# Borders of 256 in TensorE's instruction stream and the order of SyncE's transfers, in a multi-query attention kernel

## The chip, the cores and the metric

The kernel runs on one core of one Trainium2 chip. The metric is the time of one execution in device microseconds; before the change it is the median of three runs. All data are fp32.

## What is computed

64 batches of 128 tokens with 512 channels pass through a residual attention layer with 16 heads of 64 channels that share one set of keys and values (multi-query), plus one null key and value:

```python
xn = layernorm(x, g_in)
q = (xn @ Wq).reshape(b, n, H, DH).transpose(0, 2, 1, 3) * scale
k, v = split(xn @ Wkv)                    # one head for all
k = concatenate([null_kv[0], k]); v = concatenate([null_kv[1], v])
sim = einsum('bhid,bjd->bhij', q, k) + bias     # causal, then key mask
attn = softmax(sim)
out = einsum('bhij,bjd->bhid', attn, v) @ Wo
return x + layernorm(out, g_out)
```

The inputs are x (64 x 128 x 512), a bias of 16 x 128 x 128, the null key and value, a mask of 64 x 128, both gains and the weights Wq (512 x 1024), Wkv (512 x 128) and Wo (1024 x 512).

## The kernel before

The order of the instructions is written out by hand (`tc.manual_schedule()`): each engine executes its instructions in the order in which the Python code records them. Semaphore waits between engines and for buffers are put in by the framework. SyncE (SP) issues nearly all DMAs, in program order too: where one of its DMAs has to wait, those behind it wait as well.

The batches are worked on in pairs. `cycle(c)` (c from 1 to 33) mixes the stages of several pairs, with b0 = 2c:

- softmax of the pair b0, b0 + 1, whose scores the cycle before left (`scores_max`, `exps`, `rinv`, `scale`, `blocks_T`);
- output products of the pair p = b0 - 2 (`out_one`), and normalization, gain, residual and `store` of the pair r = b0 - 4;
- query products of a group two cycles ahead (`q_one`) and keys and values of batches b0 + 6 and b0 + 7 (`key_values`);
- statistics, normalization and transposition of the tokens of the batches m = b0 + 10 and m + 1 (`norm_stats`, `norm_apply`, `tokens_T`);
- at its end `region(c)`: the scores of the next pair (`heads`, L539, 64 small matmuls in program terms) and the values of the present pair (`values`, L648, 56 of them). On TensorE the region is one run of short instructions between stretches of large products.

Query and output products use Strassen's scheme with seven products (numbered 1 to 7; 4 is the last), spread over the cycle. An fp32 matmul of the program is four TensorE instructions: two weight loads and two matmuls. A full cycle has 64 + 56 + 28 + 28 + 8 matmuls (scores, values, queries, output, keys and values), so 736 such instructions, and about six separate semaphore waits. Query products end with cycle 29, keys and values with cycle 28.

Four batches form a group (GB = 4) for transfers that change the layout. They go out to DRAM and come back in another shape:

- `tokens_out` (L335, xd<-xb) and `tokens_in` (L343, xT<-xd, four DMAs) for the transposed tokens;
- `keys_T`: a VectorE transpose (kb), then L396 kd<-kb, and four DMAs L402 kT<-kd;
- `values_spread`: L379 vd<-kvt, and four DMAs L383 vr<-vd.

Each of these functions issues the way out and the way back one behind the other, so that SyncE stands at the way back until the way out has landed. All of them are called at the end of even cycles, ahead of `region(c)`, together with `load_mask`; the residual loads (`load_res`, two buffers) and the next token loads (`load_x`, three buffers) are called there in every cycle. The output tiles y have three buffers, so the DVE addition that fills a y half (L755) waits until an older y has been stored (L797).

## Time and profile before

| | |
|---|---|
| runs | 1105.44, 1102.42, 1107.50 us; median 1105.44 |
| profiled execution, its own time | 1109.08 us |
| span from the first to the last instruction in it | 1107.3 us |
| mean granted TensorE clock | 0.986 |
| busy: TensorE, VectorE, ScalarE, GpSimd | 1050.6, 764.0, 679.3, 708.0 us |
| DMA | 105.05 MB, mean 95 GB/s |
| instruction packets on q8 | 93 of together 1.52 MB |

The page gives busy times for each engine, and the chain of work that ended last. A row of the windows view is: stretch in us from the span's start, its length, then busy us and number of instructions for PE (TensorE's matmuls), PEld (its weight loads), DVE (VectorE), ACT (ScalarE) and POOL (GpSimd), then the granted clock, the mean busy share of the DMA engines and GB/s. A row of the timeline is: start, length, engine, line, operation, tiles written and read, and in brackets the idle time before it and what ended it. A row of the source view gives a count and the shortest, median and longest time in ns, and the first and last start in us. PEldq is TensorE's sequencer, SPq SyncE's.

### The profile page before, as it was taken

Reading aid. Unit: us, or ns where it says so; the run is one execution under the profiler, and the core shown is the slowest. Engines: PE = TensorE matmul, PEld = TensorE weight load, DVE = VectorE, ACT = ScalarE, POOL = GpSimd, SP = SyncE. Lnnn points to the kernel's source line nnn. Section 1 sums busy time; section 2 is a strip of 40 time slices with the busy share of each in tenths; the row PEclk is TensorE's granted clock in tenths of the full one; section 3 lists DMA queues with packets and bytes.
Section 4 is the critical chain, followed back from the end, with each engine's and each line's share of the span. In section 5 each row is a group of like instructions: output and inputs, shape, how many; then the busy total and the mean of one; then the engine's idle time right before and its main releaser. Section 6 shows DMA issues by size and latency. Waiting matters only on the chain.

```text
span 1107.3 us, 30317 instructions
## 1 busy us (share of the span) xinstructions
PE 1050.6 (95%) x11856; PEld 908.5 (82%) x11856; DVE 764.0 (69%) x1654; ACT 679.3 (61%) x2822; POOL 708.0 (64%) x530
## 2 busy tenths in 40 slices
PE   9999999999999999999999999999999999999765
PEld 8888888787888888888887888887888887888554
DVE  6776766667677777776777777776776676666563
ACT  3656567654677665567664667765557764556662
POOL 3786576484776767577574766757576575656642
PEclk9999999998999999999999999999999999999899
DMA  6641241413315042241514324142341504111111
GB/s 202 158 125 53 97 133 52 138 49 121 110 52 164 32 140 85 97 136 50 147 48 129 95 82 142 50 128 68 115 118 62 157 26 136 50 66 51 39 39 58
DMA packets 68686, 105.05 MB, mean 95 GB/s; under 512 B 8640, under 2 KB 32832, under 8 KB 66752
## 3 DMA queue, kind: packets, MB, share of 16 engines
q1 hardware_dynamic: 67440, 102.08, 30.1%
q8 instruction: 93, 1.52, 0.6%
q10 hardware_dynamic: 1104, 1.05, 0.3%
q14 instruction: 49, 0.40, 0.1%
HBM read 67.45 MB, written 35.65 MB: 93 GB/s over the span
## 4 chain that ended last, share of the span: by engine, by line
PE 76%; ACT 9%; DMA 5%; DVE 4%; issue 3%; SPq 1%; POOL 0%; DVEq 0%; ACTq 0%; POOLq 0%
PE pa L485 15%; PE pyX L736 15%; PE ps L539 8%; PE pc L485 8%; PE pyY L736 8%; ACT s L587 5%; PE poX L648 4%; PE pw L485 4%; PE pkv L354 4%; PE pyw L736 3%; PE pos L648 2%; DMA out_dram<-y 2%; PE pq L434 2%; DMA kd<-kb 2%; PE poY L648 2%
## 5 line engine op out<-in xcount | busy, mean ns | idle before, releaser
L587 ACT ACTIVATE s<-s,nmax 128x65 f32<-128x65 f32 (+1 forms) x1024 | 376.7, 389 | 0.0
L523 POOL TENSOR_TENSOR s<-biasp,mneg 128x1552 f32<-128x1552 f32 x64 | 206.1, 3221 | 66.1 <-DVE sb L623 61.9
L608 POOL TENSOR_TENSOR s<-s,rinv 128x512 f32<-128x512 f32 (+1 forms) x128 | 190.5, 1488 | 48.3 <-DVE rinv L604 47.7
L587 ACT ACTIVATION_READ_ACCUMULATOR s<-s,nmax 128x1 f32 x1024 | 217.6, 213 | 0.0
L719 POOL TENSOR_TENSOR yS<-oT 128x512 f32<-128x512 f32 x32 | 40.8, 1274 | 178.0 <-ACT oT L679 178.0
L679 ACT ACTIVATE oT<-poX,nv 128x256 f32<-128x256 f32 x64 | 30.4, 475 | 186.3 <-PE poX L648 105.6
L573 DVE TENSOR_TENSOR s<-ps,s 128x256 f32<-128x256 f32 (+2 forms) x224 | 119.9, 606 | 26.1 <-PE ps L539 23.8
L623 DVE STREAM_TRANSPOSE sb<-s 128x1536 f32<-128x1536 f32 x64 | 113.4, 1773 | 32.6 <-POOL s L608 32.4
L736 PE MATMUL pyX<-wo,oT 128*128 128x256 f32 x512 | 121.4, 380 | 6.0 <-ACT oT L679 3.9
L736 PE MATMUL pyX<-wT,oT 128*128 128x256 f32 x512 | 122.2, 382 | 5.1 <-POOL oT L719 5.1
L485 PE MATMUL pa<-xS,wq 128*128 128x256 f32 x480 | 123.4, 379 | 0.5 <-ACT ku L496 0.5
L578 DVE TENSOR_REDUCE nmax<-s 128x8 f32<-128x520 f32 (+1 forms) x128 | 116.2, 949 | 0.0
L736 PEld LDWEIGHTS pyX<-wo,oT 128*128 128x128 f32 x512 | 96.9, 190 | 21.1 <-ACT oT L679 5.3
L736 PEld LDWEIGHTS pyX<-wT,oT 128*128 128x128 f32 x512 | 97.9, 192 | 19.8 <-POOL oT L719 6.3
L648 PE MATMUL pos<-sb,vr 32*64 32x128 f32 (+1 forms) x1792 | 90.9, 325 | 8.5 <-issue 8.5
L485 PEld LDWEIGHTS pa<-xS,wq 128*128 128x128 f32 x480 | 88.9, 190 | 11.8 <-ACT ku L496 0.9
L539 PEld LDWEIGHTS ps<-kT,qT 64*64 64x64 f32 x4096 | 85.4, 134 | 10.4 <-issue 10.3
L539 PE MATMUL ps<-kT,qT 64*64 64x128 f32 (+1 forms) x4096 | 93.1, 245 | 0.0
L506 DVE TENSOR_TENSOR qT<-pc,ku 128x256 f32<-128x256 f32 x120 | 50.4, 420 | 59.1 <-ACT ku L496 43.4
L648 PE MATMUL poX<-sb,vr 32*64 32x128 f32 (+1 forms) x1024 | 84.8, 302 | 6.2 <-issue 5.8
L648 PE MATMUL poY<-sb,vr 32*64 32x256 f32 (+1 forms) x768 | 84.3, 350 | 5.3 <-issue 5.3
L503 ACT COPY qT<-pa 128x256 f32<-128x256 f32 x60 | 22.9, 381 | 94.6 <-PE pa L485 94.6
(89 smaller groups left out, 2260.8 us busy)
## 6 DMA issues: line engine op xcount, KB each, us to landing
x<-in_x_dram SPq DMA_DIRECT2D x64, 256.0 KB
res<-in_x_dram SPq DMA_DIRECT2D x64, 256.0 KB
out_dram<-y SPq DMA_DIRECT2D x64, 256.0 KB
xd<-xb SPq DMA_DIRECT2D x14, 1024.0 KB
xT<-xd SPq DMA_DIRECT2D x56, 256.0 KB
vr<-vd SPq DMA_DIRECT2D x64, 128.0 KB
kT<-kd SPq DMA_DIRECT2D x64, 64.0 KB
kd<-kb SPq DMA_DIRECT2D x16, 128.0 KB
```

Source lines behind the costliest of these rows:

```text
L354: nc.tensor.matmul(pkv, xT[g][:, t, kc, :], wkv[:, kc, :], start=(kc == 0), stop=(kc == KC - 1),)
L485: nc.tensor.matmul(prod[tag], w[:, kc, f * P : (f + 1) * P], t[:, :, kc, :], start=(start and kc == 0), stop=(kc == HK - 1), skip_group_ch ...
L506: nc.vector.tensor_tensor(o, p, k, ALU.add)
L523: nc.gpsimd.tensor_tensor(S[b], biasp, mneg[:, t].unsqueeze(1).broadcast_to([P, R8, ROW]), ALU.add,)
L539: nc.tensor.matmul(to[r][i * DH : (i + 1) * DH, f, :], qT[g][rows, f, t, NQ - 1 - i if hf else i], kT[g][rows, 0 : NQ if hf else NQ // 2, ...
L573: nc.vector.tensor_tensor(sv, ps, sv, ALU.add)
L578: nc.vector.tensor_reduce(nmax[b][:, hf], S[b][:, :, WITH_NULL[hf]], AX.X, ALU.max, negate=True)
L587: nc.scalar.activation(row, row, AF.Exp, bias=nmax[b][:, hf, k : k + 1], accum_out=rsum[b][:, hf, k : k + 1],)
L608: nc.gpsimd.tensor_tensor(sv, sv, rinvs.pop((b, hf)).unsqueeze(2).broadcast_to([P, R8, sv.shape[2]]), ALU.mult,)
L623: nc.vector.transpose(sb.rearrange("p j e q -> p e j q"), S[b][:, :, 1 : ROW - 1].rearrange("p e (j k) -> p e j k", k=Q),)
L648: nc.tensor.matmul(po[s][rows, half], vr[g][quad(s), j, t, :], sb[quad(s), slots, r * NF : (r + 1) * NF, :], start=start, stop=True, skip_ ...
L736: nc.tensor.matmul(prod[key], h[:, c, :], w[:, c, :], start=(start and c == 0), stop=(c == HC - 1), skip_group_check=not start,)
```

## The change

1. **Alignment.** `nc.tensor.addr_align(256, offset=223)` stands ahead of the last output product of every cycle up to c = 31, and `addr_align(256, offset=231)` ahead of the last query product before `region(0)`. It makes the loader fill TensorE's stream with empty instructions until the next one lies that many places behind a multiple of 256. The product behind it has 16 instructions (8 before `region(0)`), so that the region begins 239 or 240 places behind a border, and the next border lies 16 or 17 instructions into it. 32 alignments are added.
2. **Sent at the end of even cycles:** keys (kd), values (vd), then tokens (xd), with no transfer back between them.
3. **Fetched at the start of the next, odd cycle:** kT, vr, the mask of the group after, xT. Ahead of `region(0)` the fetches are left to cycle 1 in the same way.
4. **Token loads** move from the end of a cycle to the start of the next one: in SyncE's order they stand behind the sends. **Residual loads** move from the end of the cycle to the middle, behind the store of the pair r.

The orders of VectorE, ScalarE and GpSimd stay as they are; TensorE's order differs by the alignments alone, and it has 203 separate waits in place of 245. The numbers of DMAs and of bytes are the same.

```diff
-    def values_spread(g):
-        vd = dp.tile([P, GB * DH], FP, tag="vd", name=f"vd_{g}")
-        nc.sync.dma_start(out=vd, in_=kvts[g][:, 1].rearrange("p t d -> p (t d)"))
+    def values_send(g):
+        vds[g] = dp.tile([P, GB * DH], FP, tag="vd", name=f"vd_{g}")
+        nc.sync.dma_start(out=vds[g], in_=kvts[g][:, 1].rearrange("p t d -> p (t d)"))
+
+    def values_fetch(g):
         vr[g] = hp.tile([P, NQ, GB, DH], FP, tag="vr", name=f"vr_{g}")
...
-    def keys_T(g):
+    def keys_send(g):
         kb = hp.tile([P, 2, GB, Q], FP, tag="kb", name=f"kb_{g}", bufs=1)
...
+    def keys_fetch(g):
         kT[g] = hp.tile([P, NQ, GB, Q], FP, tag="kT", name=f"kT_{g}")
...
 # cycle(c), at its start
+        first = c % 2 == 0
+        for b in (m, m + 1):
+            if b < B:
+                load_x(b)
+        if not first:
+            kg = (b0 + 5) // GB
+            if kg < NG:
+                keys_fetch(kg)
+                values_fetch(kg)
+            if kg + 1 < NG:
+                load_mask(kg + 1)
+            if (m - 2) // GB < NG:
+                tokens_in((m - 2) // GB)
...
             store(r + 1)
+        if pair:
+            load_res(p)
+            load_res(p + 1)
         q_one(c, 1, 1)
...
         q_one(c, 4, 1)
+        if soft:
+            nc.tensor.addr_align(256, offset=223)
         out_one(p, 4)
-        if pair:
-            load_res(p)
-            load_res(p + 1)
-        for b in (m + 2, m + 3):
-            if b < B:
-                load_x(b)
-        if toks and m % GB == 2:
-            tokens_out(m // GB)
-            tokens_in(m // GB)
-        if c % 2 == 0:
+        if first:
             kg = (b0 + 7) // GB
             if kg < NG:
-                keys_T(kg)
-                values_spread(kg)
-            if kg + 1 < NG:
-                load_mask(kg + 1)
+                keys_send(kg)
+                values_send(kg)
+            if toks:
+                tokens_out(m // GB)
         region(c)
...
 # before region(0)
-    for m in (12, 13):
-        load_x(m)
...
+    key_values(7)
+    keys_send(1)
+    values_send(1)
     tokens_out(2)
-    tokens_in(2)
-    key_values(7)
-    keys_T(1)
-    values_spread(1)
+    nc.tensor.addr_align(256, offset=231)
     q_one(0, 4, 1)
```

More of the change, by code (lines that the diff above doesn't have):

```diff
@@ L374, in kv_out @@
         )
-    def values_spread(g):
-        vd = dp.tile([P, GB * DH], FP, tag="vd", name=f"vd_{g}")
-        nc.sync.dma_start(out=vd, in_=kvts[g][:, 1].rearrange("p t d -> p (t d)"))
+    vds, kds = {}, {}
+    def values_send(g):
+        vds[g] = dp.tile([P, GB * DH], FP, tag="vd", name=f"vd_{g}")
+        nc.sync.dma_start(out=vds[g], in_=kvts[g][:, 1].rearrange("p t d -> p (t d)"))
+    def values_fetch(g):
         vr[g] = hp.tile([P, NQ, GB, DH], FP, tag="vr", name=f"vr_{g}")
-        src = vd.rearrange("(j p) e -> p j e", p=Q)
+        src = vds.pop(g).rearrange("(j p) e -> p j e", p=Q)
         for s in range(NQ):
@@ L394, in keys_T @@
         )
-        kd = dp.tile([P, 2, GB * Q], FP, tag="kd", name=f"kd_{g}")
+        kds[g] = dp.tile([P, 2, GB * Q], FP, tag="kd", name=f"kd_{g}")
         nc.sync.dma_start(
-            out=kd.rearrange("p c e -> p (c e)"), in_=kb.rearrange("p c t q -> p (c t q)")
+            out=kds[g].rearrange("p c e -> p (c e)"),
+            in_=kb.rearrange("p c t q -> p (c t q)"),
         )
+    def keys_fetch(g):
         kT[g] = hp.tile([P, NQ, GB, Q], FP, tag="kT", name=f"kT_{g}")
-        src = kd.rearrange("(i p) c e -> c p i e", p=Q)
+        src = kds.pop(g).rearrange("(i p) c e -> c p i e", p=Q)
         for s in range(NQ):
@@ L1060 @@
     norm_stats(6)
-    keys_T(0)
-    values_spread(0)
+    keys_send(0)
+    keys_fetch(0)
+    values_send(0)
+    values_fetch(0)
     norm_nmr(6)
@@ L1084 @@
     load_late()
-    load_mask(2)
     key_values(4)
```

## The prediction

> **What bounds the kernel now.** First the page's busy times and queues, then the span cut into stages; shown are the middle and the end.

> ```profile
> span 1107.3 us, 30317 instructions
> PE 1050.6 (95%) x11856; PEld 908.5 (82%) x11856; DVE 764.0 (69%) x1654; ACT 679.3 (61%) x2822; POOL 708.0 (64%) x530
> q8 instruction: 93, 1.52, 0.6%
> ...
> 63.78:1019.11 955.33, 931.41 (x10657) 808.15 (x10656) 671.65 (x1451) 605.84 (x2544) 634.31 (x459) 0.99 0.31 95
> 1019.11:1107.30 88.19, 57.51 (x761) 45.85 (x760) 45.79 (x91) 42.55 (x173) 38.45 (x31) 0.92 0.12 43
> ```

> TensorE (second number of a stage row) bounds the 955 us in the middle; the last 88 us are bound by a chain through ScalarE. The middle is 29 regions (scores of two batches, then values of two) and the 28 stretches of large products between them. The windows of all 29 regions, and of all 28 stretches, each with their sum:

> ```profile
> 194.54:203.68 9.14, 6.70 (x242) 5.16 (x241) 7.79 (x15) 0.37 (x1) 2.33 (x1) 0.91 0.41 147
> 263.13:271.48 8.35, 6.49 (x242) 5.08 (x241) 7.78 (x15) 0.88 (x3) 2.32 (x1) 0.93 0.41 157
> 331.85:337.21 5.36, 5.36 (x242) 4.78 (x241) 5.36 (x11) 0.37 (x1) 2.32 (x1) 1.00 0.55 186
> 526.01:533.38 7.37, 5.72 (x242) 4.91 (x241) 7.37 (x15) 0.38 (x1) 2.37 (x1) 1.00 0.45 162
> 592.54:600.56 8.02, 6.03 (x242) 4.93 (x241) 7.79 (x15) 0.38 (x1) 2.30 (x1) 1.00 0.45 159
> 659.78:665.15 5.37, 5.37 (x242) 4.78 (x241) 5.37 (x11) 0.37 (x1) 2.34 (x1) 1.00 0.52 184
> 920.88:928.76 7.88, 5.63 (x242) 4.75 (x241) 7.79 (x15) 0.37 (x1) 2.34 (x1) 1.00 0.47 171
> sum 185.36, PE 166.31 PEld 140.74 DVE 168.90 ACT 11.93 POOL 117.44; mean PE 5.73 PEld 4.85 DVE 5.82 ACT 0.41 POOL 4.05
> ...
> 203.68:230.68 27.00, 27.00 (x128) 23.57 (x128) 16.25 (x39) 21.07 (x87) 17.11 (x14) 0.97 0.45 130
> 237.04:263.13 26.09, 26.09 (x130) 22.92 (x129) 17.07 (x41) 20.63 (x87) 17.95 (x15) 1.00 0.16 52
> 271.48:300.40 28.92, 28.92 (x129) 24.92 (x129) 16.29 (x39) 20.57 (x86) 17.15 (x14) 0.90 0.46 122
> 533.38:560.22 26.84, 26.44 (x129) 22.91 (x128) 17.43 (x42) 20.61 (x87) 17.72 (x14) 1.00 0.48 136
> 600.56:628.33 27.77, 27.77 (x128) 24.10 (x128) 16.26 (x39) 20.97 (x87) 17.16 (x14) 0.94 0.47 128
> 928.76:956.53 27.77, 27.77 (x128) 24.09 (x128) 14.14 (x30) 19.67 (x85) 18.03 (x12) 0.94 0.38 107
> sum 744.89, PE 740.54 PEld 646.37 DVE 486.88 ACT 574.70 POOL 499.99; mean PE 26.45 PEld 23.08 DVE 17.39 ACT 20.52 POOL 17.86
> ```

> The same work takes 5.36 us in one region and 9.14 in another; a stretch takes 26.09 us undisturbed, up to 28.92 otherwise. Inside the 9.14 us region, TensorE's timeline:

> ```profile
> 194.54 2.91 PE L539 MATMUL ps<-kT,qT 64*64 64x128 f32 x128
> ...
> 199.05 0.37 PE L648 MATMUL poY<-sb,vr 32*64 32x256 f32 x1
> 201.87 0.51 PE L648 MATMUL poY<-sb,vr 32*64 32x256 f32 x1 [2.44 <-issue]
> ```

> "Issue" means that nothing the profile shows was waited for. What ran out is instructions: TensorE's 23,712 records and 245 separate waits over the 93 packets of q8 make about 257 a packet. Counted in the program's order, the longest such idles stand at instructions 4290, 5826, 13250 and 20674, whole multiples of 256 apart. A region is 480 instructions at some 11 ns each (the 256 of the scores in 2.9 us), so it always crosses a border and mostly two; the block behind the second is asked for only at the first, under 3 us earlier. Placing those borders in all regions: seven of the 29 take 5.36 to 5.37 us, namely those whose first border lies between 26 instructions ahead of the start and 34 behind it. At 46 to 59 behind, 0.3 to 0.7 us are lost, and later ones lose up to 3.8. A border near the start is reached early, because the sequencer runs ahead while large products execute:

> ```profile
> L539 PEld LDWEIGHTS ps<-kT,qT x92: 129/135/135, 428.3 to 430.0; 64*64 64x64 f32 x92
> L539 PEldq EVENT_SEMAPHORE  x2: 51/51/51, 424.7 to 425.2; - x2
> L354 PEldq EVENT_SEMAPHORE  x2: 51/51/51, 416.7 to 416.8; - x2
> ```

> Here it reached the region's first wait at 424.7, 3.6 us before the region ran.

> **Alignment, gain in the regions.** The border then falls 16 or 17 instructions into each region, inside the clean band; two of the seven clean regions (331.85 and 659.78) were clean with DMA over half busy (the last share in the row), so the cover holds under load. The price if it doesn't is the rival of colliding sends. I take 5.36 us for all: 185.36 - 29 x 5.36 = 29.9 us.

> [...]

> **Gain in the stretches.** 744.89 - 28 x 26.09 = 14.4 us. The stretches behind the four longest regions (9.14, 8.35, 8.02, 7.88 us) ran at granted clocks of 0.90 to 0.97 and lost 0.91, 2.83, 1.68 and 1.68: 7.1 us that follow from the stalls and go with them. The other 7.3 lie in odd cycles and come from SyncE's queue:

> ```profile
> 513.32 5.48 SPq L797 DMA_DIRECT2D out_dram<-y  x2
> ...
> 527.03 0.42 SPq L335 DMA_DIRECT2D xd<-xb  x1
> 535.48 1.75 SPq L343 DMA_DIRECT2D xT<-xd  x4
> 537.33 0.38 SPq L396 DMA_DIRECT2D kd<-kb  x1
> 542.99 1.74 SPq L402 DMA_DIRECT2D kT<-kd  x4
> ...
> 548.95 3.30 SPq L797 DMA_DIRECT2D out_dram<-y  x2
> ...
> 553.64 0.42 DVE L755 TENSOR_TENSOR y<-pyY,kyu 128x256 f32<-128x256 f32 x1 [1.47 <-DMA out_dram<-y]
> ...
> PE pc L485 <- DVE qT L506: 0.4, 1, 0.4
> ```

> SyncE's own queue, around the even region at 526.01 (column two of a merged row is the time over all its issues). SyncE stands at xd's landing (8.4 us) and at kd's (5.7), so the first store of the odd cycle leaves at 548.95. A clean cycle (5.36 + 26.09 us) after its like, at 513.32, would be 544.8. So its y buffer comes free late, VectorE waits 1.47 us, and TensorE 0.4. Now kd, vd and xd leave back to back, with no wait between; two x loads follow; then kT, vr, mask and xT (13 issues of some 0.43 us, as before) wait only for what has had time to land. With kd and vd (0.26 MB) ahead of the 1.05 MB that took 8.4 us, xd lands some 2 us later, so xT leaves near 538 and the queue is free near 540, almost five us before the stores. Queued behind xd's landing are only xT and those stores. The new last dates:

> ```profile
> L354 PE MATMUL pkv<-wkv,xT x16: 272/275/275, 551.5 to 554.1; 128*128 128x128 f32 x16
> L279 DVE BATCH_NORM_STATS2 st<-x x2: 684/684/684, 546.7 to 547.7; 128x6 f32<-128x512 f32 x2
> ```

> xT is read first at 551.5 and x at 546.7, two us earlier once the region before (7.37 us) is clean: 549.5 and 544.7. I estimate xT landed by 546 (538 and the 7.5 us that passed between its first issue and kd's landing behind it) and x by 541 (0.52 MB more at xd's pace). kT and vr are read a region later (560), the mask later still. VectorE's and TensorE's work that would wait if these dates failed is everything of the odd cycle behind the first statistics and the first key product. Residual loads move ahead, past nothing but SyncE's own next loads. VectorE's, ScalarE's and GpSimd's orders do not change. So I take all 7.3, under a cover of 3 to 5 us; beyond it each late us costs a us in 14 odd cycles.

> **Alignment, its price.** An alignment fills with empty instructions. A full cycle has 736 matmul instructions and about 6 waits, so 26 are filled to reach 768. Cycle 29 lacks keys and values (60 filled), cycles 30 and 31 also the query products (169 each), and the first place takes about 53. No row shows an empty instruction. Bounds: under nothing is excluded, since it adds work to the sequencer; nothing at all if the border costs no issue time; 51 ns, a wait's own time in the rows above; and about 110 ns, the pitch of two waits in a row (416.7 to 416.8, starts 0.11 apart). I take 80 ns, midway between the two waits' figures, the nearest rows.

> The 26 cost 2.1 us (2.9 at 110 ns) under a lead of about 3.5: nothing, in the middle. The 53 and 60 exceed it by 0.7 and 1.3 us. The 169 have no lead:

> ```profile
> 1043.12 3.75 PE L736 MATMUL pyY<-wo,oT 128*128 128x256 f32 x8 [4.12 <-DVE y L755]
> 1046.66 2.85 PE L736 MATMUL pyX<-wT,oT 128*128 128x256 f32 x8
> ...
> 1072.86 3.46 PE L736 MATMUL pyY<-wo,oT 128*128 128x256 f32 x8 [4.12 <-DVE y L755]
> 1076.16 1.89 PE L736 MATMUL pyX<-wT,oT 128*128 128x256 f32 x8
> ```

> The filling stands between pyY and pyX. The sequencer is released together with pyY, so 169 x 0.08 = 13.5 us run against 3.5 us of pyY: 10.0 us, twice, and the whole chain of the end hangs on the region that follows. Idle that long lowers the granted clock; at the 1.7 us a case that the stretches above paid, 3.4. Sum 0.7 + 1.3 + 20.0 + 3.4 = 25.4 us. At 51 ns it is 13.7, at 110 ns 39, at nothing 0.

> [...]

> **Sum.** 29.9 + 7.1 + 7.3 - 25.4 = 18.9 us less. The profiled execution took 1109.08 us (span 1107.3 and 1.8 around it), 3.6 above the median of 1105.44; the difference carries over: 1086.5 us.

> **The rivals.**

> Dear filling (slower). Place: the two 169s, and beyond about 133 ns the 26s of every cycle, whose lead of 3.5 us then runs out. It takes back all 44.3 at about 121 ns each (2 x 16.9 + 3.4 + 2.9 + 3.8). At 150 ns: 43.7 + 3.4 + 4.5 + 5.5 + 28 x 0.4 = 68 us, so 1129. For it: the pitch of 110 is close below. Against: an empty instruction has no semaphore to look at. 0.10.

> The sends collide. kd, vd and xd (1.28 MB) and two x loads now start together at each even region; if half the region gain and the 7.3 go, 22 are left against 25.4: 1109. For it: the longest stalls are in regions with DMA over 0.4 busy. Against: 331.85 and 659.78, clean at 0.55 and 0.52. 0.05.

> The idles are not the fetch. If blocks are always in time and the idles in values have another cause, they stay wherever the border lies, and the clock's losses with them; only 7.3 is won and the filling is paid: 1105.4 - 7.3 + 25.4 = 1123.5. For it: the profile names no cause. Against: the spacing by 256 and the seven clean regions. 0.03. [...]

> The alignment places nothing (no filling reaches the stream). Then only the queue's 7.3: 1098. 0.06.

> **How the numbers follow.** The forecast's case has 0.76; its own ends are 1061 (filling free) and 1100 (110 ns). The range goes from 1061 to 1104, leaving out 0.18 above. About 0.5% (5.5 us) is what a measurement here tells from no change. Faster: 0.72 of the forecast's case and the 0.06 that places nothing, 0.78. Within: 0.04 of the forecast's case, near 110 ns, and 0.03 of the collision, 0.07. Slower: the dear filling, the rule and the rest of the collision, 0.15.

> **What would show it.** Right: all middle regions at 5.4 us with no idle put down to issue; q8 at about 98 packets (25,160 / 256); stretches 26.1 with no clock below 1.0; stores in odd cycles leaving 19 to 20 us after the region's start. The price is read in the last 88 us: idle before pyX of about 10 us, twice, divided by 169. Wrong: regions still uneven, pkv waiting for xT, or idle before pyX in every cycle.

## The result, and the profile after

The changed kernel takes 1090.24 us (median of 4 runs, 1089.82 to 1090.59) where the kernel before, beside it, takes 1103.93 (4 runs, 1101.96 to 1107.5): a ratio of 0.9872, 95% interval 0.9843 to 0.9901. 1086.5 had been forecast, with a range of 1061 to 1104. The profiled execution took 1090.41 us.

The busy times and the queue of instructions on the page of the changed kernel:

```profile
span 1088.6 us, 31412 instructions
PE 1032.4 (95%) x11856; PEld 901.8 (83%) x11856; DVE 760.7 (70%) x1654; ACT 676.8 (62%) x2822; POOL 707.7 (65%) x530
q8 instruction: 98, 1.61, 0.7%
```

98 packets of instructions, as foretold: the filling is in the stream. Next the windows: the span in three stages (region(0) now starts at 66.20 us, region(29) at 980.04), then two of the 29 regions with their sum, then one of the 28 stretches with theirs.

```profile
0.00:66.20 66.20, 61.49 (x440) 53.83 (x440) 46.49 (x113) 30.97 (x105) 37.37 (x43) 1.00 0.54 157
66.20:980.04 913.84, 911.43 (x10657) 801.21 (x10656) 668.39 (x1450) 603.26 (x2544) 633.21 (x458) 1.00 0.33 100
980.04:1088.63 108.59, 59.49 (x761) 46.72 (x760) 45.78 (x91) 42.53 (x173) 37.11 (x30) 0.84 0.10 35
...
192.28:197.64 5.36, 5.36 (x242) 4.78 (x241) 5.36 (x11) 0.37 (x1) 2.32 (x1) 1.00 0.61 222
223.73:229.09 5.36, 5.36 (x242) 4.78 (x241) 5.06 (x10) 0.37 (x1) 5.28 (x4) 1.00 0.18 52
...
sum 155.87, PE 155.87 PEld 138.83 DVE 147.15 ACT 10.80 POOL 110.07; mean PE 5.37 PEld 4.79 DVE 5.07 ACT 0.37 POOL 3.80
...
134.74:160.82 26.08, 26.08 (x128) 22.91 (x128) 18.51 (x44) 20.62 (x87) 17.04 (x14) 1.00 0.54 150
...
sum 730.80, PE 730.76 PEld 641.43 DVE 505.38 ACT 573.26 POOL 504.91; mean PE 26.10 PEld 22.91 DVE 18.05 ACT 20.47 POOL 18.03
```

The region that took 9.14 us takes 5.36, with the DMA engines 0.61 busy. The regions sum to 155.87 (185.36 before), the stretches to 730.80 (744.89), at a clock of 1.00. The middle is 41.5 us shorter; the start is 2.4 longer, the end 20.4 (108.59 against 88.19). TensorE's timeline shows both:

```profile
65.17 1.10 PE L492 MATMUL pa<-xS,wq 128*128 128x256 f32 x4 [1.90 <-issue]
...
978.15 1.97 PE L743 MATMUL pyX<-wT,oT 128*128 128x256 f32 x8 [1.86 <-issue]
...
1003.08 3.48 PE L743 MATMUL pyY<-wo,oT 128*128 128x256 f32 x8 [4.12 <-DVE y L762]
1015.48 2.05 PE L743 MATMUL pyX<-wT,oT 128*128 128x256 f32 x4 [8.92 <-issue]
...
1042.47 2.57 PE L743 MATMUL pyY<-wo,oT 128*128 128x256 f32 x8 [4.11 <-DVE y L762]
1054.86 1.62 PE L743 MATMUL pyX<-wT,oT 128*128 128x256 f32 x3 [9.83 <-issue]
```

The four idles put down to issue are the fillings of 53, 60, 169 and 169. From the start of pyY to the start of pyX are 12.40 and 12.39 us, filled with 169 empty instructions: 73 ns each. The trace of the changed kernel has a row for every one of them, by the source view of the line of the alignment, in a window around the first of these fillings:

```profile
L1016 PEldq NOP  x169: 13/13/13, 1003.1 to 1015.4; - x169
```

Each lasts 13 ns in the record, and 169 of them in these 12.3 us again make 73 ns from one to the next. The 26 in every cycle between show no idle.

### The profile page after: what moved, and what is told of

It reads as the page before. It is cut to its first block, busy times and chain, and to the rows that moved or that the text cites. A ratio compares the mean times of both kernels' runs of the same rounds, so it can differ in the third digit from the quotient of the medians.

```text
span 1088.6 us, 31412 instructions
## 1 busy us (share of the span) xinstructions
PE 1032.4 (95%) x11856; PEld 901.8 (83%) x11856; DVE 760.7 (70%) x1654; ACT 676.8 (62%) x2822; POOL 707.7 (65%) x530
## 3 DMA queue, kind: packets, MB, share of 16 engines
q8 instruction: 98, 1.61, 0.7%
q10 hardware_dynamic: 1104, 1.05, 0.3%
## 4 chain that ended last, share of the span: by engine, by line
PE 89%; ACT 6%; issue 3%; DMA 1%; DVE 1%; POOL 0%; ACTq 0%
PE pyX L743 19%; PE pa L492 19%; PE pyY L743 10%; PE pc L492 9%; PE ps L546 8%; PE pkv L354 5%; PE pw L492 5%; PE poX L655 4%; PE pyw L743 4%; ACT s L594 3%; PE pq L441 2%; PE pos L655 2%; PE poY L655 1%; ACT oT L686 1%; DMA x<-in_x_dram 1%
## 5 line engine op out<-in xcount | busy, mean ns | idle before, releaser
L594 ACT ACTIVATION_READ_ACCUMULATOR s<-s,nmax 128x1 f32 x1024 | 221.7, 216 | 0.0
L743 PE MATMUL pyX<-wT,oT 128*128 128x256 f32 x512 | 125.1, 388 | 26.0 <-issue 20.6
L492 PEld LDWEIGHTS pa<-xS,wq 128*128 128x128 f32 x480 | 88.9, 190 | 13.8 <-issue 2.1
L655 PE MATMUL pos<-sb,vr 32*64 32x128 f32 (+1 forms) x1792 | 81.4, 323 | 0.0
L655 PE MATMUL poY<-sb,vr 32*64 32x256 f32 (+1 forms) x768 | 79.6, 349 | 0.0
L797 DVE TENSOR_TENSOR yn<-yn,gob 128x512 f32<-128x512 f32 x64 | 43.9, 686 | 50.7 <-ACT yn L794 50.6
```

What stands on the lines that cost most here:

```text
L492: nc.tensor.matmul(prod[tag], w[:, kc, f * P : (f + 1) * P], t[:, :, kc, :], start=(start and kc == 0), stop=(kc == HK - 1), skip_group_ch ...
L594: nc.scalar.activation(row, row, AF.Exp, bias=nmax[b][:, hf, k : k + 1], accum_out=rsum[b][:, hf, k : k + 1],)
L655: nc.tensor.matmul(po[s][rows, half], vr[g][quad(s), j, t, :], sb[quad(s), slots, r * NF : (r + 1) * NF, :], start=start, stop=True, skip_ ...
L743: nc.tensor.matmul(prod[key], h[:, c, :], w[:, c, :], start=(start and c == 0), stop=(c == HC - 1), skip_group_check=not start,)
```

## The experiments

The theory: three separate effects, namely block fetches that come late in the regions, stores that leave SyncE late, and the empty instructions. Rivals: the stalls come from the transfers and not from the borders' places; the end is bound by something else than the filling.

In all kernels below the whole computation is done.

### One half of the change at a time

Alignment alone (e1_align_only): the transfers as before, both alignments added. Order alone (e2_order_only): the changed kernel without them.

```diff
-        if soft:
-            nc.tensor.addr_align(256, offset=223)
...
-    nc.tensor.addr_align(256, offset=231)
```

> The alignments with the transfers in the order of the kernel before. Theory (two separate gains: regions from the alignment, odd stretches from SyncE's order): all regions 5.37 us as in the changed kernel, the odd stretches keep their loss of about 0.5 us each (7.3 us in 14), so about 1090.2 + 7.3 = 1097.5 us. Rival (one gain: the odd stretches lost because the region ahead of them stalled, and SyncE's order does nothing): 1090. Second rival (with regions short the old order costs more, since the same transfers have less time before their readers): above 1100, with TensorE waiting for transfers.

> The transfers in the changed order, no alignment. Theory: the regions stall as in the kernel before, by where their borders fall (29.9 us over 29 regions, and the halved clock behind the longest), only the odd stretches' 7.3 us go: about 1103.9 - 7.3 = 1096.6 us, and nothing is filled at the end. Rival (the stalls in the regions came from transfers that were busy beside the block fetches, so moving them away is enough): regions near 5.4 us, and without the filling at the end about 1090 - 20 = 1070 us.

Alignment alone: 1106.01 us against 1104.63 before (ratio 1.0021, 1.0000 to 1.0043). Order alone: 1079.69 (0.9795, 0.9749 to 0.9842), 10.5 us less than the full change. The first theory (1097.5 and 1096.6 us) failed in both. Of the rivals, the second one for alignment alone came true: above 1100 us, because with short regions the old order costs more. The rival for the order alone came half true: moving the transfers shortens the regions, but not to 5.4 us. The sums of the windows, regions ahead of stretches, with alignment alone:

```profile
sum 155.65, PE 155.65 PEld 138.67 DVE 137.33 ACT 10.81 POOL 109.98; mean PE 5.37 PEld 4.78 DVE 4.74 ACT 0.37 POOL 3.79
...
sum 747.94, PE 736.66 PEld 640.32 DVE 515.22 ACT 573.49 POOL 505.33; mean PE 26.31 PEld 22.87 DVE 18.40 ACT 20.48 POOL 18.05
```

and with the order alone:

```profile
sum 169.41, PE 163.94 PEld 140.58 DVE 159.76 ACT 10.84 POOL 118.47; mean PE 5.65 PEld 4.85 DVE 5.51 ACT 0.37 POOL 4.09
...
sum 732.57, PE 731.32 PEld 641.30 DVE 495.54 ACT 574.59 POOL 499.04; mean PE 26.12 PEld 22.90 DVE 17.70 ACT 20.52 POOL 17.82
```

Alignment alone cleans all regions. But the stretches, 730.5 undisturbed (28 x 26.09), then lose 17.4 us to the late stores, not 7.3: in the kernel before, part of SyncE's lateness had passed while TensorE stalled anyway. The stores leave as late as before, 22.6 us behind the start of an even region (151.38 and 128.76) against 22.9, but the work that waits for them now comes earlier. VectorE's waits for stores in alignment alone (total, times, longest), and one such stretch in its timeline:

```profile
DVE y L755 <- DMA out_dram<-y: 25.5, 12, 3.0
...
155.91 0.42 DVE L755 TENSOR_TENSOR y<-pyY,kyu 128x256 f32<-128x256 f32 x1 [3.02 <-DMA out_dram<-y]
...
156.48 1.97 PE L736 MATMUL pyY<-wo,oT 128*128 128x256 f32 x8 [1.38 <-DVE rinv L604]
...
158.84 1.13 PE L485 MATMUL pc<-xT,wS 128*128 128x256 f32 x4 [0.40 <-DVE qT L506]
```

VectorE waits 3.02 us for a y buffer (1.47 in the row shown of before), and TensorE 1.78 behind it. In all, VectorE waits 25.5 us for stores, 13.8 in the kernel before, and in the changed kernel it has no such wait. The order alone cleans the stretches and also takes more than half of the stalls: 169.41 - 29 x 5.36 leaves 14.0 of 29.9 us. Where these 16 us lie is told by the sums of the regions of even cycles, and then of odd ones, in the kernel before:

```profile
sum 101.93, PE 86.98 PEld 73.21 DVE 97.36 ACT 6.16 POOL 36.85; mean PE 5.80 PEld 4.88 DVE 6.49 ACT 0.41 POOL 2.46
...
sum 83.43, PE 79.33 PEld 67.53 DVE 71.53 ACT 5.77 POOL 80.59; mean PE 5.67 PEld 4.82 DVE 5.11 ACT 0.41 POOL 5.76
```

With the order alone they are 85.45 and 83.96. So in sum the order shortens the even regions alone, in which the tokens are sent. The next pairs look for the cause.

### Where the order acts on the stalls

All regions with the same border, 168 or 169 instructions in, under the changed order and under that of before (both without alignment in cycles 30 and 31):

```diff
-        if soft:
-            nc.tensor.addr_align(256, offset=223)
+        if soft and c < 30:
+            nc.tensor.addr_align(256, offset=71)
...
-    nc.tensor.addr_align(256, offset=231)
+    nc.tensor.addr_align(256, offset=79)
```

> The changed kernel, but each region begins 87 past a border, so that its first border lies 168 or 169 instructions in (no alignment in cycles 30 and 31; the first place fills 157). Theory (a region stalls where it asks for its second block, and the sends of keys, values and tokens leave too late in the region to hold that request up): every region stalls by about the same 0.6 to 1.1 us, odd and even cycles alike, as the regions of the order-only kernel with borders at 147 to 177 did. With 0.75 x 29 = 22 us and 104 more empty instructions at the start (7.6 us) on the 1069.7 us of the kernel without late filling: about 1099. Rival (the border's place does nothing once the order is changed): regions of 5.37 us, 1077.

> The same border at 168, with the transfers in the order of the kernel before. Theory (in even-numbered regions of cycles whose tokens leave at the region's start, the request for the second block queues behind that 1 MB): about 1.0 us a region where no tokens leave and 2.5 to 3.8 us where they do, that is some 15 x 1.0 + 14 x 3 = 57 us; with the clock's halves behind the long ones about 40 us above the kernel with the same border in the changed order, 1135 to 1145. Rival (the order does not act on the stalls; the order-only kernel's regions were shorter since its borders lie elsewhere): regions as in the changed order, and only the odd stretches longer, by 17 us: 1116.

1109.79 us (ratio 1.0055, 1.0028 to 1.0082) and 1150.76 (1.0424, 1.0383 to 1.0466). The first is 11 above its number: its stalls come to about 1.06 us a region where 0.75 was expected, which makes 9 of the 11. The start came out as expected: 157 empty instructions cost 9.73 us of idle against 1.90 for 53, so 7.8 for the 104 more. The second is 41.0 above the first, where about 40 had been expected. The rivals of both (1077 and 1116) fell. What tells the theories apart is the sum of the 15 regions of even cycles, in which tokens leave (in all but the last), and that of the 14 of odd ones. Changed order, even then odd:

```profile
sum 95.66, PE 90.86 PEld 74.72 DVE 92.33 ACT 5.60 POOL 30.67; mean PE 6.06 PEld 4.98 DVE 6.16 ACT 0.37 POOL 2.04
...
sum 90.58, PE 83.69 PEld 69.10 DVE 83.99 ACT 5.23 POOL 87.84; mean PE 5.98 PEld 4.94 DVE 6.00 ACT 0.37 POOL 6.27
```

Order of before, even then odd:

```profile
sum 122.98, PE 94.71 PEld 76.19 DVE 111.03 ACT 5.59 POOL 30.82; mean PE 6.31 PEld 5.08 DVE 7.40 ACT 0.37 POOL 2.05
...
sum 89.95, PE 83.28 PEld 68.53 DVE 82.54 ACT 5.22 POOL 87.40; mean PE 5.95 PEld 4.90 DVE 5.90 ACT 0.37 POOL 6.24
```

Per region 6.38 and 6.47 us in the changed order, 8.20 and 6.43 in the old. So with the first border at 168 a region loses about 1.1 us whatever the order, and in the old order the even ones lose 1.8 more. Without region(0), which ran at granted clocks of 0.82 and 0.73 behind the filling at the start, and without the last, where no tokens leave, it is 2.1 (8.40 against 6.31 over 13 regions). SyncE's queue around one even region of each kernel (started at 340.19 in the old order, 335.80 in the changed), old order first:

```profile
340.55 0.53 SPq L127 DMA_DIRECT2D x<-in_x_dram  x1
341.18 0.42 SPq L335 DMA_DIRECT2D xd<-xb  x1
```

```profile
337.05 0.33 SPq L400 DMA_DIRECT2D kd<-kb  x1
337.43 0.43 SPq L381 DMA_DIRECT2D vd<-kvt  x1
337.90 0.46 SPq L335 DMA_DIRECT2D xd<-xb  x1
```

The first border comes 1.9 us into the region (169 of some 11 ns). That the second block is asked for there is read from the packets of queue 8, whose place goes with the border's: in the kernel before the packet starts 0.2 to 1.4 us behind the border in the twelve odd regions whose border lies some 70 to 240 instructions in, and with the border at 16 or 17 (the changed kernel) 1.0 to 1.6 us ahead of the start of the 13 even regions between region(0) and the last. In the old order the 1 MB of tokens (xd) left at 1.0 us, ahead of the request; in the changed order at 2.1, behind it. In the region shown the block's packet starts 5.02 us into the region in the old order (queue 8 has none from 340.24 to 345.20, one by 346.20) and 2.46 in the changed (none from 335.80 to 338.20, one by 341.00). The kernel before shows the same in one run: in the four even regions with the border some 170 to 220 instructions in, where the tokens leave at 0.91 to 0.98 us, the packet starts at 4.86 to 5.06 us; in the six odd ones with the border at some 170 to 240, where no tokens leave, at 2.76 to 3.23.

Whether it is that one send was tried on the kernel without alignment, by turning round the three sends (e9_xd_first):

```diff
+            if toks:
+                tokens_out(m // GB)
             if kg < NG:
                 keys_send(kg)
                 values_send(kg)
-            if toks:
-                tokens_out(m // GB)
```

> The order-only kernel (no alignment) with the tokens' send moved ahead of the keys' and the values'. Theory (the tokens' 1 MB is what the block fetch waits for; in the changed order it leaves 2 us into the region, when most regions have asked for their second block): it leaves about 1 us earlier again, and regions with the first border more than 100 behind the start stall by 1.3 to 3.8 us in every other cycle, as in the kernel before; in all some 10 us more than the order-only kernel's 1079.7, about 1090. Rival (what counts is that stores, residuals and x loads are no longer beside the region, not the order of the three sends): within 2 us of 1079.7.

1098.09 us (0.9949, 0.9927 to 0.9971), 18.4 more than with the order alone: the rival fell, and the theory's 10 us were too few. The same region in both, with instruction for instruction the same borders (173 in), tokens first and then tokens last, from the timelines of SyncE's queue and TensorE:

```profile
195.29 0.33 SPq L335 DMA_DIRECT2D xd<-xb  x1
...
201.69 0.42 PE L655 MATMUL pos<-sb,vr 32*64 32x256 f32 x1 [2.43 <-issue]
```

```profile
195.25 0.45 SPq L335 DMA_DIRECT2D xd<-xb  x1
...
198.57 0.42 PE L655 MATMUL pos<-sb,vr 32*64 32x256 f32 x1 [0.51 <-issue]
```

These regions start at 194.34 and 193.14, so the tokens leave 0.95 and 2.11 us in; the idle is 2.43 against 0.51. In the kernel before, the like region (from 194.54) has tokens at 0.98 us, the block's packet on queue 8 at 5.01 and an idle of 2.44. The sums of the windows over the even regions, again tokens first and then last:

```profile
sum 95.80, PE 85.06 PEld 72.63 DVE 90.97 ACT 5.61 POOL 36.21; mean PE 5.67 PEld 4.84 DVE 6.06 ACT 0.37 POOL 2.41
```

```profile
sum 85.45, PE 83.56 PEld 72.26 DVE 83.12 ACT 5.62 POOL 36.74; mean PE 5.57 PEld 4.82 DVE 5.54 ACT 0.37 POOL 2.45
```

That is 10.4 of the 21.9 us between the two profiled spans (1100.3 and 1078.4), about what was expected of the stalls. The stretches take 9.9 more, which was not expected. TensorE's waits, tokens first and then last, name about half of it:

```profile
PE pa L492 <- issue: 5.5, 3, 2.4
```

```profile
PE pa L492 <- issue: 0.4, 1, 0.4
```

These three idles stand at the first large products behind even regions of 5.36 and 5.37 us: counted in the program's order, the next border comes a few instructions behind the region there, and the same stall falls into the stretch. The rest goes with the granted clock, 0.986 and 0.992 over the two profiled executions, so 15.4 and 8.6 us of clock not granted (1100.3 x 0.014 and 1078.4 x 0.008), part of them inside regions (0.95 and 0.91 in those of 8.80 and 8.91 us). In the kernel before, the clock granted from 271.48 to 275.48 us, behind the 8.35 us region, is 0.50.

So what made the stalls long is shown: block fetches that come late behind the tokens' send. Why a fetch of one block (16 KB, by 1.61 MB in 98 packets) waits for a transfer on another queue is not.

### The price of the filling

Cycles 30 and 31 without alignment (e3_no_late_fill), and with the filling jumped over (e4_branch_over):

```diff
-        if soft:
+        if soft and c < 30:
```

```diff
-            nc.tensor.addr_align(256, offset=223)
+            nc.tensor.addr_align(
+                256, offset=223, max_nops=0 if c >= 30 else 255
+            )
```

> The changed kernel without the alignments in cycles 30 and 31 (169 empty instructions each). Theory (the filling is paid in full at the end): the idles of 8.92 and 9.83 us ahead of pyX go, and the halved clock behind them; regions 30 and 31 may stall by 1 to 2.6 us each, as in the kernel before. About 1090.2 - 18.8 - 2 + 2 = 1071 us, between 1068 and 1075. Rival (the chain of the end is bound elsewhere, and the idle moves to another wait): above 1083.

> The alignments of cycles 30 and 31 stay, but the empty instructions are jumped over by a branch. Theory (the time at these places is that of 169 instructions issued one after the other): the idles of 9 to 10 us shrink to that of one branch, so within 2 us of the kernel without these two alignments, about 1070. Rival (the time is that of fetching another block, which the border would cost however one gets there): the idles of about 9 us stay, 1090. Between: a branch throws away what was fetched ahead, and each costs a fetch of about 2.5 us, 1075.

1069.70 us (0.9713, 0.9674 to 0.9752) and 1069.38 (0.9708, 0.9670 to 0.9746). Both as the theory has it: 20.5 and 20.9 less than the full change. Where pyX had waited 8.92 us, the timeline of the first and then that of the second shows

```profile
1004.41 3.75 PE L743 MATMUL pyY<-wo,oT 128*128 128x256 f32 x8 [4.12 <-DVE y L762]
1007.95 0.63 PE L743 MATMUL pyX<-wT,oT 128*128 128x256 f32 x1
```

```profile
1003.97 3.75 PE L743 MATMUL pyY<-wo,oT 128*128 128x256 f32 x8 [4.12 <-DVE y L762]
1007.51 1.06 PE L743 MATMUL pyX<-wT,oT 128*128 128x256 f32 x2
```

with pyX right behind pyY in both. TensorE shows no idle for the branch, which stays within one block here.

How much filling a cycle hides was measured with 282 empty instructions in four cycles (e8_more_fill):

```diff
+        if c in (10, 11, 14, 15):
+            nc.tensor.addr_align(256, offset=224)
+        if soft and c < 30:
             nc.tensor.addr_align(256, offset=223)
```

> The changed kernel without the alignments of cycles 30 and 31, with 282 empty instructions in place of 26 in cycles 10, 11, 14 and 15. Theory (73 ns each, as at the end, and a lead of the sequencer of about 3.5 us to hide them): 282 x 0.073 - 3.5 = 17.1 us of idle ahead of a large product in each of the four, and the clock halved behind it; about 1069.7 + 68 + 4 x 1.7 = 1145. Rival (the lead is the 1.9 to 2.5 us that the 53 and the 60 leave of 3.9 and 4.4): 18.4 us each, about 1150. Second rival (empty instructions in mid-stream issue faster, since nothing behind them is waited for): idles under 12 us.

One run: 1152.54 us. A row of TensorE's timeline in cycle 10:

```profile
398.63 3.75 PE L743 MATMUL pyX<-wT,oT 128*128 128x256 f32 x8 [17.99 <-issue]
```

The idle is 17.95 to 18.00 us in all four places, between the two figures: 282 x 0.0733 = 20.7 less a lead of 2.7 us. A cycle thus hides some 37 empty instructions; it has 26.

### The filling jumped over everywhere

The changed order (e7_branch_all) and that of before (e11_branch_old_order), both with

```diff
-            nc.tensor.addr_align(256, offset=223)
+            nc.tensor.addr_align(256, offset=223, max_nops=0)
...
-    nc.tensor.addr_align(256, offset=231)
+    nc.tensor.addr_align(256, offset=231, max_nops=0)
```

> The changed kernel with every alignment jumped over by a branch in place of the empty instructions. Theory (a branch costs no more than a few empty instructions, since its target lies in the same or the next block): regions clean at 5.37 us as before, the 2.4 us at the start (53 empties) and the 2 us ahead of pyX in cycle 29 (60) go as well, so 1069.4 - 4.4 = 1065 us. Rival (a branch empties what the sequencer has read ahead; its lead of some 3.5 us ahead of the region is lost, and the regions or the products ahead of them stall in every cycle): 29 x 0.5 or more above 1069, so over 1083.

> The transfers in the order of the kernel before, all alignments jumped over by a branch. Theory (the alignment alone, without the price of its filling, takes away the 29.8 us in the regions and the 7 us of halved clock, but the odd stretches then lose 17.5 in place of 7.3 us, as in the align-only kernel): 1106.0 - 2.4 - 2 - 20.4 = about 1081, so order and alignment are each worth some 24 us alone and 40 together. Rival (the two are one gain and overlap): under 1070.

1063.99 us (0.9639, 0.9616 to 0.9662) and 1079.85 (0.9801, 0.9772 to 0.9829), both within 1.2 us of the theory, and the rivals fell. The first beats both kernels: 26.2 us, 2.4%, under the full change. Its windows, with the stage at the end and the sums of regions and stretches:

```profile
975.07:1061.02 85.95, 55.58 (x761) 44.83 (x760) 45.77 (x91) 42.54 (x173) 38.52 (x31) 0.94 0.13 44
...
sum 155.58, PE 155.58 PEld 138.61 DVE 146.93 ACT 10.82 POOL 109.93; mean PE 5.36 PEld 4.78 DVE 5.07 ACT 0.37 POOL 3.79
...
sum 730.79, PE 730.77 PEld 641.44 DVE 507.47 ACT 573.51 POOL 507.80; mean PE 26.10 PEld 22.91 DVE 18.12 ACT 20.48 POOL 18.14
```

It has the regions and stretches of the full change, without what the filling cost at the start, in cycle 29 and at the end. The branches themselves, by the source view:

```profile
L1016 PEldq COMPARE_BRANCH  x31: 163/163/179, 90.1 to 1026.5; - x31
```

A branch takes as long as a little over two empty instructions (163 ns, and 73), and TensorE's waits in this kernel have none for issue. So, freed of the filling's price, the alignment alone is worth some 24 us, the order alone some 25, and both together 40 (1103.9 to 1104.6 before, 1079.85, 1079.69, 1063.99). They overlap in the even regions, where each of them removes the long stalls: the alignment asks for the block earlier, the order sends the tokens later.

## Why the prediction came out as it did

In spans it met its sum: 18.7 us less (1107.3 to 1088.6) where 18.9 had been worked out. Part of that is luck, as the terms show:

- **Regions**, 29.9: 29.5 measured, but the order alone would have taken 16 of them. That the border's place decides whether a region stalls is shown by the clean regions at 16 and by 6.4 us at 168. The cover under load held. With the border at 168 in place of 16 or 17, and nothing else moved in the middle, the regions sum to 186.2 us (95.66 + 90.58) in place of 155.9.
- **Stretches**, 14.4: 14.1 measured, but the split into 7.1 and 7.3 does not stand as two independent gains. With clean regions the late stores cost 17.4.
- **SyncE's cover of 3 to 5 us** failed. The step said that kT, vr and mask wait only for what has landed. In the changed kernel vr's issues stand for x loads, by the view of SyncE's own waits (total, times, longest) and by its timeline around the even region at 507.07:

```profile
SPq L387 <- DMA x<-in_x_dram: 65.6, 26, 3.2
...
514.04 7.80 SPq L387 DMA_DIRECT2D vr<-vd  x4
...
522.42 1.80 SPq L343 DMA_DIRECT2D xT<-xd  x4
525.81 5.49 SPq L804 DMA_DIRECT2D out_dram<-y  x2
```

  xT left 15.3 us into the region, not 12. The stores left at 18.7, as early as wanted, and the lost cover cost little; the kernel without late filling, where TensorE's waits name it, shows 0.5 us at two places:

```profile
PE pkv L354 <- DMA xT<-xd: 0.5, 2, 0.3
```

- **Filling**, 25.4 at 80 ns: it came to 24.9 (2.4 at the start, 2.1 in cycle 29, 20.4 at the end). An empty instruction is 73 ns; the two 169s cost 18.75 of idle instead of 20.0; the 53 and 60 exceeded the lead by 1.90 and 1.86 instead of 0.7 and 1.3, since the lead is 2.0 and 2.5 us there (53 x 0.0733 - 1.90 and 60 x 0.0733 - 1.86; 2.7 in the four cycles above) and not 3.5. Of the 3.4 for the clock, 1.65 is left (20.4 - 18.75); behind the first 169, from 1015.48 to 1017.50 us, the granted clock is 0.50. That the sum is only 0.5 us off is luck: the end cost 3.0 less than reckoned (20.4 for 23.4), the start and cycle 29 together 2.5 more (4.5 for 2.0).
- **"The difference carries over"** is the step that failed. The profiled execution of before, 1109.08, lies at the upper end of its runs (1098.66 to 1109.50 beside the experiments), and what puts it there goes with the change: the new kernel's runs lie within 0.8 us. Against medians the gain is 13.7 us, so the result is 3.7 above the forecast. The kernels in which the block's packet starts late behind the tokens' send spread most (before 10.8 us, tokens first 9.0); with the alignment alone it is 4.2, with the branches in the changed order 1.7. The slower runs of before also have the lower granted clock, from 0.991 at 1098.66 us to 0.983 at 1109.50. That the stalls make the spread fits this, but was not tried by itself, and the kernels had different numbers of runs (39 of before, 5 to 10 of the others).

Of the rivals, dear filling, idles that are not the fetch, and an alignment that places nothing are excluded by the 73 ns, the border at 168 and the 98 packets. The collision of sends had the right resource and the wrong sign: the tokens' send did collide with the fetches, in the kernel before, and the change moved it behind them. The row spoken for it, long stalls in regions with DMA over 0.4 busy, was the trace of that, and the prediction used it only as a risk. It therefore credited the alignment with all 29.9 us, of which the order alone removes 16, and did not see that the alignment as built loses to leaving it out.

## What to carry to other kernels

Where a dense burst of short instructions stalls with nothing waited for, count the instructions to the block borders (256 apart here), and look at which large transfer leaves just ahead of the request for the next block; in the kernel without alignment, sending 1 MB a microsecond later (2.11 in place of 0.95 us into the region) took 18.4 us off. Fill with a branch (tried here only with its target in the same block), or only where the engine's sequencer has a lead to hide the filling; here that was 2.0 to 2.7 us at the start and in the middle, and at the end only the 2.6 and 3.5 us of pyY, against 12.4 of the 169. Before adding up gains, try each half alone: a stall may be hiding another engine's lateness, as here 17.4 us in place of 7.3.
